# Splitting the first part's weights by tap halves, so that four passes can leave out an image row

## The chip, the cores and the metric

One core of one Trainium2 chip. The metric is the time of one execution on the device in microseconds; the median of three runs of the kernel before is 2496.78 us (2495.84 to 2496.85).

## The reference

Input `x` is (4, 32, 32, 16): four images of 32 x 32 pixels with 16 channels. Four residual layers are applied, each to a group-normalised copy of `x`. Three of them (layers 0, 1 and 3) are of this kind:

```python
first = einsum('ijyx,byxc->bijc', M, inputs)
kern = ...                       # G: for each pixel (i,j) its own 3x3 kernel, 16 -> 16 channels
shifted = conv(inputs, kern)     # (b, i, j, y, x, f): 1024 convolutions of the whole image
diff = relu(inputs[:, None, None] - shifted)
second = einsum('ijyx,bijyxc->bijc', W, diff)
x = x + first - second
```

The third kind (layer 2, "interval") pools over intervals of the image with running maxima and minima and makes two small dynamic-programming steps of sigmoid and maximum over 33 x 33 tables. What fills the time is `shifted`: for each of the 1024 pixels, 16 output channels and 4 images, a 3 x 3 x 16 convolution over 1024 places.

## The kernel before, in words

**Phases, steps, units.** The four images are two groups of two (`g`, `b`). A phase is one convolution layer on one group: six phases in the order (g0, L0), (g1, L0), (g0, L1), (g1, L1), (g0, L2), (g1, L2), where L2 is the reference's layer 3. A phase has 8 chunks `t` of 128 output pixels; a chunk has 32 steps, one for each channel `f` and image `b`. So a phase is 256 steps, and there are 1536 in all. Four channels' weights are a unit: eight steps use one unit. Units 0 and 1 ("plain") are used as loaded, by 16 steps; units from 2 on are split.

**What a step does on TensorE.** The nine taps' 16 channels are 144 input rows. The partitions' halves 0 to 63 and 64 to 127 hold the left and right half image (512 pixels each, two adjacent matmuls of 64 rows, one into each half of the PSUM pair). Each half has two slots `s` of four taps, 0 to 3 and 4 to 7; the ninth tap stands apart in `im9`. For accuracy in the fast matmul format, weights and images are split into an upper part (the top bits) and the rest. `first_part` makes four passes of 512 columns: `WU[s]` with `iy[s]` (upper weights with upper image x 2^-12) and `WL[s]` with `iz[s]` (the rests); ScalarE then scales the PSUM pair by 1 + 2^-12 (L627). `second_part`, one step later, adds `WD[s]` with `iyz[s]` and the ninth tap (496 columns; its last image row has nothing to add), and VectorE (L644) does minimum, product with W and sum into a column of `acc`. Four PSUM pairs are in turn. Layout by weights: `WU`, `WL`, `WD` are 128 x 512 tiles of `parts[:, 0]`; `parts[:, 1]` is a copy with the partition halves swapped, made by two DMAs on SP (L242).

**The order around it.** Each engine's order is the order in which this program emits. Each step of `conv_layer` takes one piece of `prep_parts` (eight pieces for a unit, thirteen steps ahead of its first use), then emits `first_part` of this step and `second_part` of the step before, then perhaps one piece of `behind`, the generator that prepares the next phase. A piece of `prep_parts` yields a tuple: at `IDLE` ScalarE has no weight work in that step, at `CALM` VectorE has none. A piece of `behind` that yields a number is followed by the next after so many steps; one that yields `IDLE` or `CALM` waits for a step whose tuple has it. Piece k of a unit falls on steps that are k + 2 modulo 8, so the step 0 of a phase has a piece 6. The pieces before: 1 VectorE's mask of the upper bits (`upper`, L198); 2 ScalarE's half of the ninth tap's weights (L172); 3 `WD` scaled on ScalarE (L231), `WL` by subtraction on POOL (L232), the ninth tap's sum on POOL (L233); 4 `WU` copied on ScalarE (L235), `WD` summed on POOL (L236); 5 the next unit's subtraction of ones on the diagonal (`prep`, L209); 7 the swapped copy (L242) and the load of raw weights two units on (L108). Their tuples have IDLE at 1, 5, 6, 7, 8 and CALM at 6, 7, 8.

**What is behind.** `before_conv` normalises the next group (`group_norm`: sums, pause `gap`, totals with two pauses `gap`, mean and squares on POOL, pause 4, sums, pause `gap`, IDLE, ScalarE's square-root table, two pauses `gap`, pause 2, IDLE, 1/deviation, pause 2, product, pause 3; `gap` is 4, in the last layer 1, in the interval layer 2), transposes it, writes it to DRAM (`xs`, L356, 8 DMAs) and reads it back in 24 DMAs (L367), two a step, as `raw`, one image row block for each tap. After a pause of 12 (6 in the last layer) `split` makes `iy` and `iz` for each of the two images and `difference` makes `iyz`. For `first` of the reference, `load_first_terms` loads M (4 MB, `MT`, two DMAs on SP, L385) and `first_terms` multiplies. `interval_layer` runs the interval layer for a group; its `step` adds 33 x 33 tables on POOL (L550) and takes maxima on VectorE, one row of tables every six steps.

**The shared buffer.** One buffer of 128 x 8192 float32 (pool `big`, `bufs=1`) holds in turn the plain units, `MT` and the interval layer's tables; a new tile there waits for the readers of the last.

**Queues.** All of the DMAs named go out on SP's queue, in the order of the program.

Of the kernel before, what the change touches and what calls it, by code (L numbers as in the profile page):

```python
# [15 lines left out]
P = 128  # L16
B, H, C = 4, 32, 16
NG = 2
# [11 lines left out]
LAST = (H - 1) * HW  # L30
ROWS = P // H
# [11 lines left out]
def net_kernel(ctx: ExitStack, tc: tile.TileContext, x, xq, xi, convs, iv_w, iv_b, out):  # L43
# [77 lines left out]
    iy = [const.tile([P, 2, GB, NH], F32R, name=f"iy{g}") for g in range(NG)]  # L121
    iz = [const.tile([P, 2, GB, NH], F32R, name=f"iz{g}") for g in range(NG)]
# [8 lines left out]
    plain = first[:, : PLAIN * 3 * FU * P].rearrange("p (u s f k) -> p u s f k", u=PLAIN, s=3, f=FU)  # L131
# [29 lines left out]
    pick = (ident[:, 4 * C : 5 * C], ident[:, :C])  # L161
# [21 lines left out]
    def zeros(g):  # L183

        nc.gpsimd.memset(xt[g], 0.0)
        for y in (0, HP - 1):
            nc.gpsimd.dma_start(
                xs[g][:, :, y * WP : (y + 1) * WP], zero[:GC].rearrange("p (h n) -> p h n", h=2)
            )

# [24 lines left out]
    def prep_parts():  # L215

        for u in range(PLAIN, n_chunks * NU):  # L220
            parts = wpool.tile([P, 2, 3, FU, P], F32R, tag="parts", bufs=AHEAD + 1, name=f"parts_{u}")
            W9 = wpool.tile([P, FU, P], F32R, tag="W9", bufs=AHEAD + 1, name=f"W9_{u}")
            units[u] = [parts[:, :, k] for k in range(3)] + [W9]
            src = raws.pop(u)
            w8 = src[:, 0].rearrange("p f k -> p (f k)")
            WU, WL, WD = (parts[:, 0, k].rearrange("p f k -> p (f k)") for k in range(3))
            high = upper(src[:, 0:1], 1, f"w{u}")[:, 0]
            yield (IDLE,)
            halve(W9, src[:, 1], low_w)
            yield ()  # L230
            nc.scalar.activation(WD, high, AF.Copy, scale=-EPS)  # L231
            nc.gpsimd.tensor_tensor(WL, w8, high, ALU.subtract)  # L232
            nc.gpsimd.tensor_tensor(W9, W9.bitcast(F32), src[:, 2], ALU.add)  # L233
            yield ()
            nc.scalar.copy(WU, high)  # L235
            nc.gpsimd.tensor_tensor(WD, WD.bitcast(F32), WL.bitcast(F32), ALU.add)  # L236
            yield ()
            prep(u + 1)
            yield (IDLE,)
            yield (IDLE, CALM)  # L240
            for h in range(2):
                nc.sync.dma_start(  # L242
                    parts[64 * h : 64 * h + 64, 1].bitcast(F32),
                    parts[64 - 64 * h : 128 - 64 * h, 0].bitcast(F32),
                )
            load_raw(u + RAWS)
            yield (IDLE, CALM)
            yield (IDLE, CALM)
# [12 lines left out]
    def split(eng, g, b, name, pause=IDLE):  # L261

        high = upper(image(raw[:, :2, b], WP), 2, f"x{name}{b}")
        yield 1
        for s in range(2):
            eng.tensor_tensor(
                image(iz[g][:, s, b], HW), image(raw[:, s, b], WP), image(high[:, s], HW), ALU.subtract
            )
            yield pause
            nc.scalar.activation(iy[g][:, s, b], high[:, s], AF.Copy, scale=EPS)  # L270

    def difference(eng, g, b, s):
        eng.tensor_tensor(
            iyz[g][:, s, b], iy[g].bitcast(F32)[:, s, b], iz[g].bitcast(F32)[:, s, b],
            ALU.subtract,
        )
# [66 lines left out]
    def before_conv(g, layer):  # L343
# [17 lines left out]
        for slot, row, tap in [(tap // 4, tap % 4, tap) for tap in range(8)] + [  # L361
            (2, row, 8) for row in range(4)
        ]:
# [7 lines left out]
        yield 6 if layer == 2 else 12  # L371
        for b in range(GB):
            yield from split(nc.gpsimd, g, b, f"{g}{layer}")
            yield IDLE
            halve(image(im9[g][:, b], HW), image(raw[:, 2, b], WP), low_x)
            for s in range(2):
                difference(nc.gpsimd, g, b, s)
            yield 3
# [211 lines left out]
    def products(ps, pairs, first, ninth=False):  # L590


        for k, (w, v) in enumerate(pairs):
            n = LAST if ninth and k == len(pairs) - 1 else NH
            for h in range(2):
                r = slice(64 * h, 64 * h + 64)
                nc.tensor.matmul(  # L597
                    ps[:, h, :n],
# [5 lines left out]
                )  # L604

    def first_part(step):
# [5 lines left out]
        if u < PLAIN:  # L612
# [4 lines left out]
                True, ninth=True,  # L617
# [5 lines left out]
            [(WU[:, s], iy[g][:, s, b]) for s in range(2)]  # L623
            + [(WL[:, s], iz[g][:, s, b]) for s in range(2)],
            True,
# [4 lines left out]
    def second_part(step, ps):  # L630
# [5 lines left out]
        if u >= PLAIN:  # L636
# [3 lines left out]
                False, ninth=True,  # L640
# [54 lines left out]
    def behind(phase):  # L695
# [7 lines left out]
        if phase + 1 < len(phases):  # L703
# [3 lines left out]
            terms = g1 == NG - 1 and layer1 < NL - 1  # L707
            if terms:
                mt = load_first_terms(layer1)
            yield from before_conv(g1, layer1)  # L710
            if terms:
# [24 lines left out]
    for b in range(GB):  # L736
# [9 lines left out]
        "left0": rows[:, 0, 0::3], "right0": rows[:, 1, 1:2],  # L746
        "top0": rows[:, 0, 0:3], "bottom0": rows[:, 1, 2:4],
        "left1": rows[:, 0, 2:3], "right1": rows[:, 1, 2:3],
        "top1": rows[:, 1, 0:3], "bottom1": rows[:, 0, 2:4],
# [83 lines left out]
    def rest_of_start():  # L833
# [14 lines left out]
        yield 2  # L848
        for b in range(GB):
            yield from split(nc.vector, 0, b, "00", 1)  # L850
            yield 1
            for s in range(2):
                difference(nc.vector, 0, b, s)
# [88 lines left out]
```

## Time and profile before

| | |
|---|---|
| median of 3 runs | 2496.78 us (2495.84 to 2496.85) |
| profiled execution, its own time | 2497.43 us |
| its span, first to last instruction | 2495.7 us, TensorE's granted clock 1.0 |
| TensorE busy | 2478.2 us (99%) |
| VectorE busy | 2081.2 us (83%) |
| ScalarE busy | 1882.6 us (75%) |
| POOL busy | 1103.0 us (44%) |
| share of the chain that ended last: TensorE, L597 | 94% |
| passes, L597: 512 columns, 64 rows | 6080 matmuls for each of iy, iz, iyz |
| passes, L597: 496 columns | 3072 matmuls |
| L644, VectorE, mean | 1224 ns, 1536 times |
| L627, ScalarE, mean | 1008 ns, 1520 times |

PE is TensorE's matmuls, PEld its weight loads, DVE VectorE, ACT ScalarE, SP the queue that issues the DMAs. Line numbers are those of the kernel. A busy share is an average over the span, and matmuls' ends are modelled, so that two passes can seem to overlap: the time of a pass is read from the distance of two starts.

### The profile page before, as it was taken

What the parts mean: (1) busy time and instruction counts of PE and PEld (TensorE: products, weight loads), DVE (VectorE), ACT (ScalarE), POOL (GpSimd) and SP (SyncE); (2) the same over time, 40 slices, a digit from 0 to 9 for tenths busy, and PEclk for the clock granted to TensorE, in tenths of its full rate; (3) what the DMA queues carried; (4) which work ended last, traced back from release to release, by engine and by line L of the source; (5) the groups of instructions that cost most, each with busy time, mean ns of one, the idle gap of its engine ahead of it and who ended that gap; (6) DMA issues with size and microseconds to landing.
All of it is one profiled execution on the core that took longest, in us unless ns stands there. A gap on an engine that the chain in (4) does not pass through costs nothing.

```text
span 2495.7 us, 56685 instructions
## 1 busy us (share of the span) xinstructions
PE 2478.2 (99%) x21906; PEld 2080.4 (83%) x21906; DVE 2081.2 (83%) x3617; ACT 1882.6 (75%) x2181; POOL 1103.0 (44%) x990
## 2 busy tenths in 40 slices
PE   8999999999999999999999999999999999999999
PEld 5899888888888888888888888888889888888887
DVE  9888788888888887888888988889889887788887
ACT  4777777787777777777777777787777777777776
POOL 3445333454343435433345555454646444333332
PEclk9999999999999999999999999999999999999999
DMA  5566445465444654544454444554444467354442
GB/s 176 184 150 178 116 136 143 114 177 141 132 142 133 200 160 123 140 134 133 134 144 136 136 119 138 146 159 134 125 138 137 133 167 202 114 145 136 136 136 54
DMA packets 86622, 354.43 MB, mean 142 GB/s; under 512 B 23888, under 2 KB 25808, under 8 KB 85584
## 3 DMA queue, kind: packets, MB, share of 16 engines
q1 hardware_dynamic: 85360, 350.21, 50.5%
q8 instruction: 172, 2.82, 0.5%
q14 instruction: 98, 0.80, 0.1%
q10 hardware_dynamic: 864, 0.58, 0.1%
q0 software_dynamic: 128, 0.02, 0.0%
HBM read 199.78 MB, written 1.02 MB: 80 GB/s over the span
## 4 chain that ended last, share of the span: by engine, by line
PE 95%; DMA 2%; DVE 1%; SPq 1%; issue 1%; ACT 1%; POOL 0%; DVEq 0%; ACTq 0%; POOLq 0%
PE pc L597 94%; DMA parts<-parts 1%; PE pf L395 1%; DMA raw<-in_g 1%; DVE junk L644 1%; SPq L367 0%; ACT pc L627 0%; SPq L356 0%; SPq L242 0%; PE ps_r L531 0%; PE ps_l L518 0%; DVE tables L478 0%; DMA xs<-xt 0%; ACT iy L270 0%; ACT L328 0%
## 5 line engine op out<-in xcount | busy, mean ns | idle before, releaser
L644 DVE SCALAR_TENSOR_TENSOR junk<-pc,WT 128x1024 f32<-128x1024 f32 x1536 | 1879.5, 1224 | 389.8 <-PE pc L597 347.0
L627 ACT ACTIVATE pc<-pc 128x1024 f32<-128x1024 f32 x1520 | 1531.8, 1008 | 578.4 <-PE pc L597 549.0
L597 PE MATMUL pc<-iy,parts 64*128 64x512 f32 x6080 | 957.3, 387 | 3.8 <-DMA parts<-parts 3.2
L597 PE MATMUL pc<-iyz,parts 64*128 64x512 f32 x6080 | 954.0, 387 | 2.3 <-ACT pc L627 2.2
L597 PE MATMUL pc<-iz,parts 64*128 64x512 f32 x6080 | 953.5, 386 | 0.0
L597 PEld LDWEIGHTS pc<-iyz,parts 64*128 64x128 f32 x6080 | 589.3, 184 | 110.4 <-ACT pc L627 6.1
L597 PEld LDWEIGHTS pc<-iy,parts 64*128 64x128 f32 x6080 | 590.2, 184 | 106.1 <-DMA parts<-parts 5.4
L597 PEld LDWEIGHTS pc<-iz,parts 64*128 64x128 f32 x6080 | 591.7, 184 | 104.4
L232 POOL TENSOR_TENSOR parts<-raw,upper_w 128x512 fp32r<-128x512 f32 x190 | 246.5, 1297 | 965.6 <-PE pc L597 808.8
L597 PE MATMUL pc<-im,W 64*128 64x496 f32 x3072 | 609.5, 384 | 0.0
L597 PEld LDWEIGHTS pc<-im,W 64*128 64x128 f32 x3072 | 301.2, 184 | 56.5 <-issue 3.5
L233 POOL TENSOR_TENSOR W<-W,raw 128x512 fp32r<-128x512 f32 x190 | 247.3, 1301 | 1.6 <-ACT W L172 1.6
L236 POOL TENSOR_TENSOR parts<-parts 128x512 fp32r<-128x512 f32 x190 | 246.6, 1298 | 1.9 <-ACT parts L231 1.9
L209 POOL TENSOR_TENSOR raw<-raw,ident 128x512 f32<-128x512 f32 x190 | 200.7, 1056 | 80.6 <-DMA raw<-in_g 80.5
L172 ACT ACTIVATE W<-raw,low_w 128x512 fp32r<-128x512 f32 x190 | 136.0, 716 | 0.1
L644 DVE DVE_READ_ACCUMULATOR junk<-pc,WT 128x1 f32 x1536 | 127.3, 83 | 0.0
L231 ACT ACTIVATE parts<-upper_w 128x512 fp32r<-128x512 f32 x190 | 118.6, 624 | 4.4 <-DVE upper_w L198 4.2
L235 ACT CAST parts<-upper_w 128x512 fp32r<-128x512 f32 x190 | 116.8, 615 | 0.0
L198 DVE TENSOR_SCALAR upper_w<-raw 128x512 int32<-128x512 int32 x190 | 82.1, 432 | 0.4 <-POOL raw L209 0.2
L659 POOL TENSOR_SCALAR acc<-acc 128x32 f32<-128x32 f32 x40 | 11.9, 297 | 151.4 <-DVE junk L644 146.8
L550 POOL TENSOR_TENSOR tables<-ft_b,rt 128x1089 f32<-128x1089 f32 x16 | 37.7, 2359 | 0.0
L550 POOL TENSOR_TENSOR tables<-ft_a,rt 128x1089 f32<-128x1089 f32 x16 | 37.7, 2359 | 0.0
(136 smaller groups left out, 397.3 us busy)
## 6 DMA issues: line engine op xcount, KB each, us to landing
raw<-in_g SPq DMA_DIRECT2D x190, 768.0 KB, 7.1
parts<-parts SPq DMA_DIRECT2D x380, 384.0 KB, 5.0
WT<-in_w SPq DMA_DIRECT2D x48, 512.0 KB, 4.8
MT<-in_mt SPq DMA_DIRECT2D x6, 2048.0 KB, 14.2
raw<-xs SPq DMA_DIRECT2D x120, 71.8 KB, 2.8
raw<-in_xi SPq DMA_DIRECT2D x3, 287.0 KB, 4.7
raw<-in_xi SPq DMA_DIRECT2D x1, 861.0 KB, 6.8
xs<-xt SPq DMA_DIRECT2D x40, 18.0 KB, 1.7
```

The source lines that it names most:

```text
L172: nc.scalar.activation(dst, src, AF.Copy, scale=mask[:, 1:2])
L198: nc.vector.tensor_scalar(t.bitcast(I32), src.bitcast(I32), HIGH, None, op0=ALU.bitwise_and)
L209: eng.tensor_tensor(raws[u][:, s, at:to], raws[u][:, s, at:to], pick[s][:, f0 + at : f0 + to].unsqueeze(2).to_broadcast([P, to - at, P]), ...
L231: nc.scalar.activation(WD, high, AF.Copy, scale=-EPS)
L232: nc.gpsimd.tensor_tensor(WL, w8, high, ALU.subtract)
L233: nc.gpsimd.tensor_tensor(W9, W9.bitcast(F32), src[:, 2], ALU.add)
L235: nc.scalar.copy(WU, high)
L236: nc.gpsimd.tensor_tensor(WD, WD.bitcast(F32), WL.bitcast(F32), ALU.add)
L550: nc.gpsimd.tensor_tensor(t, ft[:, i, :].unsqueeze(1).to_broadcast([P, T1, T1]), rt, ALU.add,)
L597: nc.tensor.matmul(ps[:, h, :n], lhsT=w[r], rhs=v[r] if n == NH else v[r][:, :n], start=first and k == 0, stop=k == len(pairs) - 1, skip_g ...
L627: nc.scalar.activation(ps, ps, AF.Copy, scale=1.0 + EPS)
L644: nc.vector.scalar_tensor_tensor(junk, ps.rearrange("p h n -> p (h n)"), 0.0, chunks[n], op0=ALU.min, op1=ALU.mult, accum_out=accs[phase][ ...
```

## The change

The taps' order becomes `TAPS`: slot 0 has the taps 0 to 3, slot 1 the taps 6, 7, 4, 5. In the first part's passes a group of 64 rows no longer holds four taps' upper (or lower) parts, but the upper and lower parts of two taps: `WU` holds taps 0, 1 (slot 0) or 6, 7 (slot 1) with `ia`, `WL` the taps 2, 3 or 4, 5 with `ib`. Taps 0 and 1 belong to the row above, 6 and 7 to the row below: in the passes of `WU` the outer row of the half is left out, 496 columns instead of 512. The passes of `WL` come first. The weights' quarters of 32 partitions are put together on POOL and ScalarE: two subtractions and one copy on POOL and one copy on ScalarE more for each unit, and the pieces' order differs; the swapped copy goes with piece 8, IDLE is at pieces 1, 4, 7, 8 and CALM at 4, 7, 8. The images' upper and lower parts are made in a temporary tile (in `big`) and placed into `ia` and `ib` by 12 DMAs for each image (`place`). `MT` of the first two layers is loaded after `before_conv` instead of ahead of it, with a pause of 24 steps before `first_terms`.

```diff
+TAPS = ((0, 1, 2, 3), (6, 7, 4, 5))
+TEMP = 2 * 2 * GB * NH
...
+    QUARTERS = [(slice(64 * h, 64 * h + 32), slice(64 * h + 32, 64 * h + 64)) for h in range(2)]
...
             high = upper(src[:, 0:1], 1, f"w{u}")[:, 0]
             yield (IDLE,)
-            halve(W9, src[:, 1], low_w)
+            nc.scalar.copy(WU, high)
+            nc.gpsimd.tensor_tensor(WL, w8, high, ALU.subtract)
+            for lo, hi in QUARTERS:
+                nc.gpsimd.tensor_tensor(WU[hi], w8[lo], high[lo], ALU.subtract)
             yield ()
             nc.scalar.activation(WD, high, AF.Copy, scale=-EPS)
-            nc.gpsimd.tensor_tensor(WL, w8, high, ALU.subtract)
+            nc.gpsimd.tensor_tensor(WD, WD.bitcast(F32), WL.bitcast(F32), ALU.add)
+            yield ()
+            yield (IDLE, CALM)
+            halve(W9, src[:, 1], low_w)
             nc.gpsimd.tensor_tensor(W9, W9.bitcast(F32), src[:, 2], ALU.add)
             yield ()
-            nc.scalar.copy(WU, high)
-            nc.gpsimd.tensor_tensor(WD, WD.bitcast(F32), WL.bitcast(F32), ALU.add)
+            (lo0, hi0), (lo1, hi1) = QUARTERS
+            nc.scalar.copy(WL[lo0], high[hi0])
+            nc.gpsimd.tensor_copy(WL[lo1], high[hi1])
+            prep(u + 1)
             yield ()
-            prep(u + 1)
-            yield (IDLE,)
             yield (IDLE, CALM)
             for h in range(2):
                 nc.sync.dma_start(
...
             load_raw(u + RAWS)
-            yield (IDLE, CALM)
             yield (IDLE, CALM)
...
+    def place(engs, g, b, temp):
+        ty, tz = (v.bitcast(F32) for v in halves(temp, b))
+        da, db = (v[g].bitcast(F32)[:, :, b] for v in (ia, ib))
+        k = 0
+        for h, (lo, hi) in enumerate(QUARTERS):
+            for s in range(2):
+                at = HW if s == h else 0
+                for to, src in ((lo, ty), (hi, tz)):
+                    engs[k % len(engs)].dma_start(da[to, s, :LAST], src[lo, s, at : at + LAST])
+                    k += 1
+            for to, src in ((lo, ty), (hi, tz)):
+                engs[k % len(engs)].dma_start(db[to], src[hi])
+                k += 1
+            yield 1
...
         yield 6 if layer == 2 else 12
+        temp = big.tile([P, 8192], F32R, tag="big", name=f"temp_{g}{layer}")[:, :TEMP]
         for b in range(GB):
-            yield from split(nc.gpsimd, g, b, f"{g}{layer}")
+            yield from split(nc.gpsimd, g, b, temp, f"{g}{layer}")
             yield IDLE
             halve(image(im9[g][:, b], HW), image(raw[:, 2, b], WP), low_x)
+            yield from place([nc.sync], g, b, temp)
             for s in range(2):
-                difference(nc.gpsimd, g, b, s)
-            yield 3
+                difference(nc.gpsimd, g, b, s, temp)
+            yield 1
...
-            [(WU[:, s], iy[g][:, s, b]) for s in range(2)]
-            + [(WL[:, s], iz[g][:, s, b]) for s in range(2)],
-            True,
+            [(WL[:, s], ib[g][:, s, b]) for s in range(2)]
+            + [(WU[:, s], ia[g][:, s, b]) for s in range(2)],
+            True, {2 + s: without_outer(s) for s in range(2)},
...
             terms = g1 == NG - 1 and layer1 < NL - 1
+            yield from before_conv(g1, layer1)
             if terms:
                 mt = load_first_terms(layer1)
-            yield from before_conv(g1, layer1)
-            if terms:
+                yield 24
                 yield from first_terms(layer1, mt)
...
+        temp = first.bitcast(F32R)[:, used : used + TEMP]
         for b in range(GB):
-            yield from split(nc.vector, 0, b, "00", 1)
-            yield 1
+            yield from split(nc.vector, 0, b, temp, "00", 1)
+            yield from place([nc.sync, nc.scalar], 0, b, temp)
             for s in range(2):
-                difference(nc.vector, 0, b, s)
+                difference(nc.vector, 0, b, s, temp)
             yield 1
```

In `products`, `without_outer(s)` gives a half's matmul 496 columns that begin at 16 in the half h = s and at 0 in the other. The host packs G and the first images in the order of `TAPS`.

## The prediction

> **What bounds the kernel now.** I read the page's busy shares first, then the chain that ended last.
>
> ```profile
> PE 2478.2 (99%) x21906; PEld 2080.4 (83%) x21906; DVE 2081.2 (83%) x3617; ACT 1882.6 (75%) x2181; POOL 1103.0 (44%) x990
> PE 95%; DMA 2%; DVE 1%; SPq 1%; issue 1%; ACT 1%; POOL 0%; DVEq 0%; ACTq 0%; POOLq 0%
> ```
>
> TensorE is busy throughout and holds 95% of the chain: a column taken from a pass is time, if nothing else makes TensorE wait. The timeline of TensorE (start us, duration, what) gives the price of a column.
>
> ```profile
> 1001.18 0.62 PE L597 MATMUL pc<-iy,parts 64*128 64x512 f32 x4
> 1001.64 0.62 PE L597 MATMUL pc<-iz,parts 64*128 64x512 f32 x4
> 1002.09 0.62 PE L597 MATMUL pc<-iyz,parts 64*128 64x512 f32 x4
> 1002.54 0.38 PE L597 MATMUL pc<-im,W 64*128 64x496 f32 x2
> 1002.76 0.62 PE L597 MATMUL pc<-iy,parts 64*128 64x512 f32 x4
> ```
>
> The two halves' matmuls start together, so a line with x4 is two passes. Six passes of 512 columns take 1002.54 - 1001.18 = 1.36 us, 0.227 each; the one of 496 takes 0.22. Sixteen columns are 6.7 ns, and a step is 1.58 us.
>
> Next the timeline of one weight unit (eight steps, 12.64 us), since the change gives POOL and ACT more to do for each.
>
> ```profile
> 1217.48 0.42 DVE L198 TENSOR_SCALAR upper_w<-raw 128x512 int32<-128x512 int32 x1
> 1218.03 1.30 POOL L232 TENSOR_TENSOR parts<-raw,upper_w 128x512 fp32r<-128x512 f32 x1 [7.84 <-PE pc L597]
> 1218.10 0.71 ACT L172 ACTIVATE W<-raw,low_w 128x512 fp32r<-128x512 f32 x1
> ...
> 1219.29 1.29 POOL L233 TENSOR_TENSOR W<-W,raw 128x512 fp32r<-128x512 f32 x1
> 1220.54 1.29 POOL L236 TENSOR_TENSOR parts<-parts 128x512 fp32r<-128x512 f32 x1
> 1221.78 1.04 POOL L209 TENSOR_TENSOR raw<-raw,ident 128x512 f32<-128x512 f32 x1
> 1221.99 1.10 SPq L242 DMA_DIRECT2D parts<-parts  x2
> ```
>
> I count from L198's start, called t. POOL's links begin 1.26 us apart from t = 0.55; the swap of halves (L242) is issued at t = 4.5 and lands 5.0 us later by the page's median. POOL is idle 7.84 us per unit, ACT 0.57 us ahead of most L627.
>
> Last, the place where TensorE does wait for a swap: SP's, VectorE's and TensorE's timeline at the last load of MT.
>
> ```profile
> 2067.57 2.07 SPq L385 DMA_DIRECT2D MT<-in_mt  x2
> 2069.91 0.42 DVE L198 TENSOR_SCALAR upper_w<-raw 128x512 int32<-128x512 int32 x1
> 2074.43 1.11 SPq L242 DMA_DIRECT2D parts<-parts  x2
> 2089.04 0.61 PE L597 MATMUL pc<-iy,parts 64*128 64x512 f32 x3
> 2091.01 0.50 PE L597 MATMUL pc<-iy,parts 64*128 64x512 f32 x1 [1.37 <-DMA parts<-parts]
> ```
>
> The swap was issued at t = 4.5 as always, but behind 4 MB of MT it landed 16.0 us later, 23.4 us after MT's issue. TensorE needed it for its second pass, at 2089.04 + 0.23, which is t = 19.4, and lost 1.7 us. The other two MT loads (issued at 109.02 and 822.73) show swaps that took up to 14.2 and 11.7 us; no stall followed, because MT had gone out right behind the swap before.
>
> **What is removed.** In 1520 steps, two passes lose 16 columns: 1520 x 2 x 6.7 ns = 20.3 us. That the shortened passes are shorter in fact, the 496-column row shows.
>
> **A unit's chain.** POOL gets two quarter subtractions and a quarter copy. A quarter has as many elements per partition as L232, so I take 1.26 us each for the subtractions and 1.0 for the copy (L209: 1.04); bounds 0.6 and 2.36 (L550, 1089 elements). The new chain: WL 0.55 to 1.81, two quarters to 4.3, WD to 5.6, W9 to 7.3 (its ACT half, three steps behind the first, ends at 6.0), copy to 8.3, the next unit's L209 to 9.4. All fits in 12.6 us; if it did not, its 3.5 us on 190 units would be 665 us. ACT's extra quarter copy (0.61, from L235) lies in the 0.57 us gap ahead of an L627, as L235 does now without delaying any; uncovered it would be 116 us. But the swap moves from t = 4.5 to 8.4 and lands at 14.5, not 10.6, due at 19.2: spare time falls from 8.8 to 4.7 us. And ACT's copy into WL, the fourth step after the first (t = 0.6 + 4 x 1.57 = 6.9), must wait until POOL's WD sum (end 5.6) has read WL: a new wait with 1.3 us to spare. Behind it in ACT's queue is the scaling L627, and behind that TensorE's second part; L627 ends 0.36 us before it is needed (1218.76 + 1.01 against 1220.13).
>
> VectorE and POOL side by side: L644 has a spread of only 1189 to 1227 ns over 1536 calls, whether POOL runs or not, so I charge nothing. One rule speaks against that: the Trainium skill (GPSIMD Engine Reference, Key points) says that POOL shares its SBUF interfaces with VectorE and contends with instructions in a two-port mode or with two SBUF inputs. If L644 were such an instruction, 3.5 us more of POOL per unit against VectorE's 0.35 us of idle per step would cost some (3.5 - 2.8) x 190 = 133 us; L644 reads one input from PSUM, and the row decides for nothing.
>
> **Where POOL is late for ACT.** I counted the yields. Step 0 of a phase is the sixth piece of a unit; in phases 0 and 2 the group norm's pauses (4 each, and IDLE pieces now 1, 4, 7, 8) put the second image's differences behind piece 2, so 2 x 1.3 us go ahead of the WD sum. It ends at 8.2, ACT is held 1.3 us, TensorE 1.3 - 0.36 = 0.9. The same count gives one such place in each of the five prepared images' phases: 4.7 us. In the interval layers' first step an L550 (2.36 us) stands behind piece 2 twice per layer: 4 x (2.36 - 1.3 - 0.36) = 2.8. Sum 7.5, bounds 0 (quarters at 0.6) and 12; I take 6.
>
> **The placing copies.** 12 per image on SP, 24 a phase, at L242's 0.55 us: 6.6 us of SP per image, ahead of swaps or behind them. Their landing lets the differences' buffer go; nothing on TensorE waits for them within 10 steps. Cost through the swap: 0 to 2 us a phase, inside the next item. In the start phase half go to ACT's queue (six of 0.35 to 0.57 us an image) while TensorE runs the plain units; 0.5 us, bounds -1 and 2.
>
> **The stretches of xs reads.** Five times, 24 L367 fill SP's queue; there the swaps go out up to 15 us after L198 (513.12 against 498.97) and land just at the due time: most of the page's 8.6 us of TensorE waiting for parts outside MT. The swap stands one piece later, so behind two to four more L367 of 0.45 us: 1 to 2 us in each stretch. I take 6 us, bounds 0 and 12.
>
> **MT moves.** It now needs the buffer of the temporary images, so it goes after them. The same count puts it, in phases 0 and 2, at piece 4 of a unit (steps 150 and 598), two steps behind the differences and four ahead of that unit's swap. SP reaches it when the buffer is free: between t = 6.9 (POOL's end of the differences) and 10.3 (placing copies behind a raw load). I take 8.5. The swap, ready at 11, is in SP's order behind MT. From the three MT loads now, a swap behind MT lands 22.5 to 23.4 us after MT's issue; there a raw load had gone 1.2 us ahead, here it is older, so I take 20.5, with 18.3 (MT's own landing) as lower end. Landing: 29.0, due 19.2, stall 9.8. Bounds 6 and 14.5. Two of them: 19.6 us (12 to 29). They are hidden by nothing: TensorE has no other work in its order. The 24 steps (38 us) given to MT do cover its own landing. At the last phase MT keeps its place, but the swap before it is later by up to 3.9 us: 1.5 us more (0 to 4).
>
> **The sum**, against the profiled execution's 2497.43 us (span 2495.7): - 20.3 + 19.6 + 6 + 6 + 1.5 + 0.5 = + 13.3, so 2510.7. The median of the runs is 0.65 lower: 2510.
>
> **Rivals.** (1) Faster: the swap behind MT does land in time. It decides from a landing below t = 19.2, that is if the swap's packets pass MT's. For it: 14.2 us is not 18.3, and two loads of three cost nothing. Against: they were issued after the swap before. Then the 19.6 is 0, the other terms 6 to 14: 2497.4 - 20.3 + 6 to 14, less 0.65, 2482 to 2491. (2) The waits are half of what I took, and gain and loss cancel: 2492 to 2502. (3) POOL's quarters cost 2.2 us (like L550): WD ends at 7.5, ACT is late in every unit by 0.6, TensorE by about 0.25 on 190 units: 47 us more, 2557. For it: only that no 32-partition operation of this size is in the trace.
>
> **How the numbers follow.** My forecast (both MT stalls, the small waits) has 0.64, own range 2502 to 2524; rival 1 0.13, rival 2 0.17, rival 3 0.06. The bound of what can be told is 0.2%, 5 us: faster 0.13, same 0.17, slower 0.64 + 0.06 = 0.70. The range 2492 to 2524 leaves out rivals 1 and 3, about 2 in 10.
>
> **What would show it.** TensorE's rows for the first part's two shortened forms start 0.22 apart; two waits of 6 to 14 us for the parts swap, 25 to 30 us after L198, right behind MT near 260 and 1000 us; TensorE's waits for ACT up from 8.3 us; L242 issued at t = 8.4. I am wrong if no wait for parts follows MT, or if L242 comes at t > 10 in an ordinary unit.

## The result, and the profile after

The changed kernel takes 2572.64 us (median of 5 runs, 2569.19 to 2573.68) against 2496.78 (2495.84 to 2497.15): ratio 1.0302, 95% interval 1.0287 to 1.0317. It is slower by 75.9 us where 13.3 had been forecast; the profiled span is 2570.9 us, 75.2 longer. The direction was right, the size far outside the range.

The page's busy times and its chain that ended last:

```profile
PE 2491.1 (97%) x21906; PEld 2061.6 (80%) x21906; DVE 2092.3 (81%) x3617; ACT 1989.8 (77%) x2371; POOL 1731.6 (67%) x1560
...
PE 81%; DMA 6%; DVE 4%; issue 4%; ACT 3%; POOL 3%; SPq 0%; ACTq 0%; DVEq 0%; POOLq 0%
```

TensorE held 95% of the chain and holds 81%: the path now runs through DMAs, VectorE, ScalarE and POOL. (TensorE's busy time is no lower although columns are gone: part of it ran at half clock, see below.) The saving itself is there. TensorE's timeline of an undisturbed step:

```profile
1233.82 0.62 PE L628 MATMUL pc<-ib,parts 64*128 64x512 f32 x4
1234.27 0.60 PE L628 MATMUL pc<-ia,parts 64*128 64x496 f32 x4
1234.71 0.62 PE L628 MATMUL pc<-iyz,parts 64*128 64x512 f32 x4
1235.17 0.38 PE L628 MATMUL pc<-im,W 64*128 64x496 f32 x2
1235.39 0.62 PE L628 MATMUL pc<-ib,parts 64*128 64x512 f32 x4
```

The two shortened passes (four matmuls of 64 rows, two for each half image) take 1234.71 - 1234.27 = 0.44 us, 0.22 each; the step 1235.39 - 1233.82 = 1.57 us. Over the whole trace the mean distance from one pass's start to the next, waits left out, is 0.2270 us behind 512 columns and 0.2203 behind 496: 6.7 ns for 16 columns.

POOL's part of the same unit, with the swap on SP:

```profile
1231.09 1.30 POOL L235 TENSOR_TENSOR parts<-raw,upper_w 128x512 fp32r<-128x512 f32 x1 [3.90 <-DVE upper_w L203]
1232.46 2.63 POOL L237 TENSOR_TENSOR parts<-raw,upper_w 32x512 fp32r<-32x512 f32 x2
1235.17 1.29 POOL L240 TENSOR_TENSOR parts<-parts 128x512 fp32r<-128x512 f32 x1
...
1237.98 0.61 POOL L248 CAST parts<-upper_w 32x512 fp32r<-32x512 f32 x1
1238.62 2.47 SPq L253 DMA_DIRECT2D parts<-parts  x2
```

In an ordinary unit things are nearly as reckoned: a quarter subtraction costs what a whole one costs (two in 2.63 us), the copy 0.61, the swap goes out 7.5 us after L235's start (forecast 7.85), and POOL is still idle for 3.9 us. What was lost was lost elsewhere. The table of waits (who waited for whom: us in total, times, longest), first before:

```profile
PEld pc L597 <- ACT pc L627: 6.1, 10, 0.8
...
PEld pc L597 <- DMA parts<-parts: 5.4, 5, 1.7
...
ACT parts L231 <- DVE upper_w L198: 4.2, 2, 2.1
```

and after:

```profile
PEld pc L628 <- ACT pc L664: 65.6, 81, 4.3
...
PEld pc L628 <- DMA parts<-parts: 36.9, 13, 11.5
PE pc L628 <- ACT pc L664: 34.8, 39, 3.9
...
PE pc L628 <- DMA parts<-parts: 31.4, 11, 11.1
ACT parts L234 <- DVE upper_w L203: 28.0, 30, 2.8
ACT parts L247 <- POOL parts L240: 24.5, 17, 2.4
```

By the sums that the prediction took (PEld and PE together, which wait side by side, so that no time lost can be read from them) waits for parts went from 8.6 to 68.3 us and waits for ACT from 8.3 to 100.4. The last two rows, of ACT, are where its lateness begins: L247 is the wait that the prediction named, L234 one that it did not.

From the trace I summed what the distances of neighbouring matmuls' starts have above 222 ns and sorted them by what held the second (ScalarE's by its longest idle time in the 4.5 us ahead), before and after. The rows of MT are exact to 0.1 us; the others, ScalarE's above all, move by 1 to 2.5 us with the rule of sorting:

| term | forecast | after less before |
|---|---|---|
| 16 columns in two passes | -20.3 | -20.3 (by the spacing) |
| two MT stalls | +19.6 | +25.6 |
| last MT | +1.5 | +2.9 |
| stretches of xs reads | +6 | +1.7 |
| ScalarE late | +6 | +37.4 (L247 19.3, L234 14.7, ScalarE merely busy 3.4) |
| start | +0.5 | +4.2 |
| TensorE at half clock | not named | +9.6 |
| passes right behind a wait | not named | +7.5 |
| sum | +13.3 | +68.6, of 75.2; 6.6 not assigned |

**MT.** The timeline of SP and TensorE at the first MT:

```profile
264.74 1.59 SPq L110 DMA_DIRECT2D raw<-in_g  x1
...
270.58 4.34 SPq L300 DMA_DIRECT2D ia<-temp  x4
274.96 1.29 SPq L303 DMA_DIRECT2D ib<-temp  x2
278.04 0.81 SPq L416 DMA_DIRECT2D MT<-in_mt  x2
...
278.96 1.15 SPq L253 DMA_DIRECT2D parts<-parts  x2
...
297.31 0.79 PE L628 MATMUL pc<-ib,parts 64*128 64x512 f32 x1 [10.40 <-DMA parts<-parts]
...
298.92 0.79 PE L628 MATMUL pc<-ib,parts 64*128 64x512 f32 x1 [0.82 <-DMA parts<-parts]
```

MT stands between two swaps, as forecast. The swap behind it landed 18.3 us after its issue and TensorE lost 10.6 and 1.4 us by those distances; at the second MT 11.3 and 2.4.

**ScalarE behind POOL.** Where the group norm runs, from the timeline:

```profile
70.13 0.26 POOL L348 TENSOR_SCALAR mean_c<-whole_mc 128x16 f32<-128x16 f32 x1 [5.21 <-DVE whole_mc L341]
...
71.80 1.30 POOL L235 TENSOR_TENSOR parts<-raw,upper_w 128x512 fp32r<-128x512 f32 x1
...
73.18 2.63 POOL L237 TENSOR_TENSOR parts<-raw,upper_w 32x512 fp32r<-32x512 f32 x2
...
75.89 1.30 POOL L240 TENSOR_TENSOR parts<-parts 128x512 fp32r<-128x512 f32 x1
...
77.22 0.62 ACT L247 CAST parts<-upper_w 32x512 fp32r<-32x512 f32 x1 [1.99 <-POOL parts L240]
...
78.79 0.73 PE L628 MATMUL pc<-iyz,parts 64*128 64x512 f32 x4 [1.48 <-ACT pc L664]
```

POOL stood 5.21 us for VectorE's L341 and did three small operations (L348, L350, L352) before the unit's chain could begin at 71.80. ScalarE's copy waited 1.99 us for the WD sum, the scaling L664 stood behind it, and TensorE waited 1.48.

**ScalarE behind the mask.** Another place, in the interval layer:

```profile
1995.53 2.35 POOL L581 TENSOR_TENSOR tables<-ft_b,rt 128x1089 f32<-128x1089 f32 x1
...
1995.78 2.38 DVE L203 TENSOR_SCALAR upper_w<-raw 128x512 int32<-128x512 int32 x1
...
1998.19 0.62 ACT L234 CAST parts<-upper_w 128x512 fp32r<-128x512 f32 x1 [1.76 <-DVE upper_w L203]
...
1999.78 0.73 PE L628 MATMUL pc<-iyz,parts 64*128 64x512 f32 x4 [1.26 <-ACT pc L664]
```

A mask of 0.42 us took 2.38 beside POOL's L581 and ended 0.28 us after it. The copy into WU now follows the mask by one step; before, that step held the ninth tap's half, which needs no mask.

### The profile page after: what moved, and what is told of

Its sections match the earlier page's. It is cut to its first block, busy times and chain, and to the rows that moved or that the text cites. A ratio compares the mean times of both kernels' runs of the same rounds, so it can differ in the third digit from the quotient of the medians.

```text
span 2570.9 us, 57968 instructions
## 1 busy us (share of the span) xinstructions
PE 2491.1 (97%) x21906; PEld 2061.6 (80%) x21906; DVE 2092.3 (81%) x3617; ACT 1989.8 (77%) x2371; POOL 1731.6 (67%) x1560
## 4 chain that ended last, share of the span: by engine, by line
PE 81%; DMA 6%; DVE 4%; issue 4%; ACT 3%; POOL 3%; SPq 0%; ACTq 0%; DVEq 0%; POOLq 0%
PE pc L628 79%; DMA parts<-parts 4%; DVE junk L681 3%; ACT pc L664 2%; DMA raw<-in_g 1%; POOL parts L237 1%; PE pf L426 1%; POOL parts L240 1%; DMA WT<-in_w 1%; POOL parts L235 0%; DVE upper_w L203 0%; DMA raw<-in_xi 0%; POOL iyz L289 0%; POOL W L244 0%; POOL tables L581 0%
## 5 line engine op out<-in xcount | busy, mean ns | idle before, releaser
L681 DVE SCALAR_TENSOR_TENSOR junk<-pc,WT 128x1024 f32<-128x1024 f32 x1536 | 1879.7, 1224 | 451.1 <-PE pc L628 411.8
L664 ACT ACTIVATE pc<-pc 128x1024 f32<-128x1024 f32 x1520 | 1529.3, 1007 | 476.5 <-PE pc L628 467.7
L628 PE MATMUL pc<-iyz,parts 64*128 64x512 f32 x6080 | 973.1, 391 | 35.7 <-ACT pc L664 34.8
L628 PE MATMUL pc<-ib,parts 64*128 64x512 f32 x6080 | 972.3, 389 | 32.0 <-DMA parts<-parts 31.4
L628 PE MATMUL pc<-ia,parts 64*128 64x496 f32 x6080 | 944.7, 381 | 0.0
L628 PEld LDWEIGHTS pc<-ib,parts 64*128 64x128 f32 x6080 | 595.7, 185 | 145.4 <-DMA parts<-parts 36.9
L628 PEld LDWEIGHTS pc<-iyz,parts 64*128 64x128 f32 x6080 | 584.5, 185 | 153.7 <-ACT pc L664 65.6
L628 PEld LDWEIGHTS pc<-ia,parts 64*128 64x128 f32 x6080 | 596.8, 185 | 111.4
L628 PE MATMUL pc<-im,W 64*128 64x496 f32 x3072 | 617.8, 385 | 0.0
L235 POOL TENSOR_TENSOR parts<-raw,upper_w 128x512 fp32r<-128x512 f32 x190 | 246.2, 1296 | 548.5 <-DVE upper_w L203 448.3
L237 POOL TENSOR_TENSOR parts<-raw,upper_w 32x512 fp32r<-32x512 f32 x380 | 490.7, 1291 | 28.8 <-ACT parts L234 3.3
L244 POOL TENSOR_TENSOR W<-W,raw 128x512 fp32r<-128x512 f32 x190 | 247.8, 1304 | 36.1 <-ACT W L175 34.4
L214 POOL TENSOR_TENSOR raw<-raw,ident 128x512 f32<-128x512 f32 x190 | 198.0, 1042 | 82.7 <-DMA raw<-in_g 58.5
L234 ACT CAST parts<-upper_w 128x512 fp32r<-128x512 f32 x190 | 118.3, 623 | 35.5 <-DVE upper_w L203 28.0
L247 ACT CAST parts<-upper_w 32x512 fp32r<-32x512 f32 x190 | 118.0, 621 | 30.9 <-POOL parts L240 24.5
L681 DVE DVE_READ_ACCUMULATOR junk<-pc,WT 128x1 f32 x1536 | 127.3, 83 | 0.0
L248 POOL CAST parts<-upper_w 32x512 fp32r<-32x512 f32 x190 | 116.7, 614 | 12.3
L239 ACT ACTIVATE parts<-upper_w 128x512 fp32r<-128x512 f32 x190 | 118.1, 621 | 5.9 <-DVE iyz L289 5.9
L203 DVE TENSOR_SCALAR upper_w<-raw 128x512 int32<-128x512 int32 x190 | 89.0, 468 | 0.9 <-POOL raw L214 0.7
```

The costliest lines, as they stand in the source:

```text
L214: eng.tensor_tensor(raws[u][:, s, at:to], raws[u][:, s, at:to], pick[s][:, f0 + at : f0 + to].unsqueeze(2).to_broadcast([P, to - at, P]), ...
L237: nc.gpsimd.tensor_tensor(WU[hi], w8[lo], high[lo], ALU.subtract)
L247: nc.scalar.copy(WL[lo0], high[hi0])
L628: nc.tensor.matmul(ps[:, h, at : at + n], lhsT=w[r], rhs=v[r] if n == NH else v[r][:, :n], start=first and k == 0, stop=k == len(pairs) - ...
L664: nc.scalar.activation(ps, ps, AF.Copy, scale=1.0 + EPS)
L681: nc.vector.scalar_tensor_tensor(junk, ps.rearrange("p h n -> p (h n)"), 0.0, chunks[n], op0=ALU.min, op1=ALU.mult, accum_out=accs[phase][ ...
```

## The experiments

Ratios are to the kernel before, which ran beside each version on the same chip; brackets are 95% intervals. Gains in us are differences of medians, mostly to the changed kernel's 2572.64. The kernel before took 2496.8 to 2497.7 on all the chips used, while the runs of one version spread by 1 to 10 us.

| version | us | ratio |
|---|---|---|
| cut alone, in the kernel before | 2483.31 | 0.9948 [0.9931, 0.9964] |
| MT's new place alone, in the kernel before | 2497.62 | 1.0000 [0.9990, 1.0010] |
| change, MT behind the swap | 2551.10 | 1.0212 [1.0195, 1.0229] |
| change, MT in quarters | 2539.08 | 1.0164 [1.0149, 1.0179] |
| change, both copies on POOL | 2567.97 | 1.0281 [1.0265, 1.0297] |
| change, quarters of WU copied | 2558.31 | 1.0243 [1.0229, 1.0257] |
| change, ninth tap first | 2559.32 | 1.0246 [1.0230, 1.0261] |
| change, start's copies on SP | 2575.93 | 1.0313 [1.0295, 1.0330] |
| MT in quarters + ninth first | 2517.75 | 1.0078 [1.0063, 1.0093] |
| the same, three edits more | 2501.34 | 1.0017 [1.0008, 1.0026] |
| those, and the start on SP | 2496.06 | 0.9993 [0.9984, 1.0001] |
| and the swap on POOL, behind L214 | 2505.03 | 1.0035 [1.0021, 1.0049] |
| or on POOL, ahead of L214 | 2506.59 | 1.0037 [1.0024, 1.0050] |
| or on SP, two pieces earlier | 2484.67 | 0.9949 [0.9936, 0.9963] |

### The columns by themselves

In the kernel before, the two passes over `iz` leave out their last 16 columns; nothing else changes.

```diff
-            n = LAST if ninth and k == len(pairs) - 1 else NH
+            n = LAST if ninth and k == len(pairs) - 1 or first and not ninth and k > 1 else NH
```

> The kernel before, with the two passes of iz cut to 496 columns and nothing else changed (it leaves out the last image row of those passes). Theory (a column is 0.417 ns, TensorE is the bound): 1520 x 2 x 6.7 = 20.3 us off, 2476.5 us. Rival (another engine is just behind TensorE, so that the columns are worth less): 2485 or more.

2483.31 (2481.76 to 2490.46): 14.4 us gained, between the theory and its rival. The profile, of the fastest run, has longer waits near 2025 us, where the kernel before lost 0.9 us:

```profile
2023.24 0.50 PE L597 MATMUL pc<-iy,parts 64*128 64x512 f32 x1 [0.84 <-DMA parts<-parts]
2025.02 0.79 PE L597 MATMUL pc<-iy,parts 64*128 64x512 f32 x1 [1.28 <-DMA parts<-parts]
```

And its windows view right behind (from:to, us, busy of PE, PEld, DVE, ACT, POOL, granted clock, DMA share, GB/s):

```profile
2025.02:2028.43 3.41, 3.41 (x16) 2.79 (x18) 0.43 (x1) 1.01 (x1) 0.33 (x1) 0.50 0.92 281
```

16 matmuls in 3.41 us, at half clock (0.50). Waits and half clock cost some 3.6 us. The profiled span is 15.7 us shorter, 19.3 with those given back, so the saving is nearly the 20.3 that was reckoned. But a faster TensorE brings the same swaps closer to their due times.

### MT

First, MT's new place alone, in the kernel before (no buffer to wait for):

```diff
+            yield from before_conv(g1, layer1)
             if terms:
                 mt = load_first_terms(layer1)
-            yield from before_conv(g1, layer1)
-            if terms:
+                yield 24
                 yield from first_terms(layer1, mt)
```

> The kernel before, with only MT's move: in phases 0 and 2 it is loaded after the preparation of the images, 24 steps ahead of its use; the images are made as before, with no temporary tile. Theory (MT comes between swap and swap because it must wait until the temporary tile is free; where nothing holds the buffer, SP reaches it right behind the last raw load, as before): 2496 to 2500. Rival (the place in the program's order alone makes the swap late): 2510 to 2520.

2497.62, no difference. There MT goes out at 234.17, right behind a swap (231.77) and 9.4 us ahead of the next. The place in the program costs nothing; the wait for the buffer of the temporary images does, because it carries MT to within a microsecond of the swap that comes after it.

Second, in the changed kernel, MT four steps later, so that it goes out behind that swap:

```diff
+                yield 4
                 mt = load_first_terms(layer1)
```

> The changed kernel, with a pause of 4 more steps ahead of MT's load, so that in phases 0 and 2 it stands behind a unit's swap (piece 8) instead of ahead of it (piece 4). Theory (the swap is late because it is queued behind 4 MB): the two stalls of TensorE of 12 to 14 us and the half clock behind them go, save for 1 to 2 us each: 26 to 32 us off 2572.6, so 2541 to 2547, and granted clock near 0.996. Rival (the stall is the shorter lead of the swap, wherever MT stands): 2565 or more.

2551.10, 21.5 us gained, short of the 26 to 32 expected. The stalls of 12.0 and 13.6 us shrank to 1.6 and 3.7. They did not vanish: the next swap still landed 12 to 15 us after its issue behind 4 MB. At the last MT, whose place is the same, the loss grew from 4.5 to 6.6. Third, MT as four loads of 1 MB, eight steps apart, each behind a swap, in the last phase too:

```diff
-        for half in range(2):
-            nc.sync.dma_start(mt[:, NT // 2 * half : NT // 2 * (half + 1)], convs[layer][0][half])
+        for q in range(4):
+            nc.sync.dma_start(
+                mt[:, 2 * q : 2 * q + 2], convs[layer][0][q // 2][:, q % 2 * 2 : q % 2 * 2 + 2]
+            )
+            yield 8
```

> The changed kernel with each MT load in four DMAs of 1 MB, eight steps apart, each right behind a unit's swap and raw load; in the last phase too. Theory (a swap is late by what is queued ahead of it): no TensorE stall for parts behind MT, all three gone, and no half clock but the start's: 24 to 34 us off 2572.6, so 2539 to 2549, and 3 to 8 below the kernel that only moved MT behind the swap (2551). Rival (MT's 4 MB cost the same wherever they go): 2550 or more.

2539.08, 33.6 us gained, as expected (24 to 34). Its waits for parts:

```profile
PEld pc L631 <- DMA parts<-parts: 10.6, 9, 2.1
```

So MT, with the half clock and the passes behind its stalls, was worth 33.6 of the 96 us that the change lost beside its 20.3 us of gain; I had 21.1.

### ScalarE's two waits

The wait of L247 for POOL can be taken from ScalarE by giving the copy to POOL:

```diff
-            nc.scalar.copy(WL[lo0], high[hi0])
+            nc.gpsimd.tensor_copy(WL[lo0], high[hi0])
```

> The changed kernel, with both quarter copies into WL on POOL, so that ScalarE no longer waits for POOL's sum of WD. Theory (that wait costs TensorE 17 stalls, 19 us): 2550 to 2556, and no wait of ScalarE for POOL L240. Rival (the same lateness reaches TensorE another way, by the swap that POOL now issues 0.6 us later): 2568 or more.

2567.97, at most a few us gained (the intervals overlap): a miss. ScalarE no longer waits for POOL, but what was lost came back in other rows: L234's share grew from 14.7 to 21.7 us and waits for parts from 36.1 to 42.7.

Next the chain's length. `WU`'s quarters have the values that `WL` has just received, so they can be copied:

```diff
-                nc.gpsimd.tensor_tensor(WU[hi], w8[lo], high[lo], ALU.subtract)
+                nc.gpsimd.tensor_copy(WU[hi], WL[lo])
```

> The changed kernel with one edit: the two quarters of WU are copied from WL's quarters, which hold the same values (so far 614 ns for a 32x512 copy on POOL), and no longer subtracted a second time (1291 ns). POOL's chain up to the sum of WD is 1.35 us shorter in each of 190 units; the order of everything else stands. Theory (ScalarE's copy into WL waits for a POOL that is late by the chain's length, 17 sites of 1.1 us each): most of the 19.3 us behind L247 goes, the masks' 14.7 us and the MT stalls stay: 2553 to 2561 us. Rival (POOL is late because group norm and tables stand ahead of the chain, its length does not matter, or the lateness moves on to the swap): 2567 us or more.

2558.31 (2550.77 to 2560.62), 14.3 us gained, within what was expected. ScalarE's waits in its profile, which is of the fastest run:

```profile
ACT parts L234 <- DVE upper_w L203: 27.0, 30, 2.7
...
ACT parts L247 <- POOL parts L240: 4.1, 7, 0.7
```

The wait for POOL fell from 24.5 to 4.1, the one for the mask stayed. The first was the chain's length on top of POOL's late start.

Then the order: the ninth tap first, which needs no mask, and L247's copy last, on POOL:

```diff
+            halve(W9, src[:, 1], low_w)
+            nc.gpsimd.tensor_tensor(WL, w8, high, ALU.subtract)
+            yield ()
             nc.scalar.copy(WU, high)
-            nc.gpsimd.tensor_tensor(WL, w8, high, ALU.subtract)
...
+            nc.gpsimd.tensor_tensor(W9, W9.bitcast(F32), src[:, 2], ALU.add)
...
-            nc.scalar.copy(WL[lo0], high[hi0])
+            nc.gpsimd.tensor_copy(WL[lo0], high[hi0])
```

> The changed kernel with the pieces' order changed: piece 2 has the ninth tap's ScalarE half and POOL's WL, piece 3 the WU copy and POOL's quarters and the ninth tap's sum, piece 5 WD, piece 6 both copies into WL on POOL. So ScalarE's first operation of a unit no longer needs VectorE's mask of one step before, and none waits for POOL. Theory (two new waits of ScalarE, for POOL and for VectorE, delay the scaling L664: 19 and 15 us): ScalarE's waits for VectorE's mask fall from 28 us to under 8, TensorE's waits for ScalarE from 100 us to under 25, and the time to 2535 to 2550. Rival (with the copies on POOL alone the lateness only moved on to the swap, 4.7 us gained; it will again): 2560 or more.

2559.32, 13.3 us gained, between the theory and its rival. The waits show why not more:

```profile
PEld pc L628 <- DMA parts<-parts: 53.5, 19, 14.7
...
PEld pc L628 <- DVE junk L681: 21.9, 37, 1.4
...
PEld pc L628 <- ACT pc L664: 17.4, 25, 5.2
...
DVE upper_w L203 <- POOL raw L214: 15.9, 23, 2.2
```

Waits for ACT fell from 65.6 to 17.4. In their place VectorE now waits for POOL's L214 in the next unit's mask, TensorE for VectorE, and the MT stalls grew from 12.0 and 13.6 to 16.6 and 15.5 us.

### The start

```diff
-            yield from place([nc.sync, nc.scalar], 0, b, temp)
+            yield from place([nc.sync], 0, b, temp)
```

> The changed kernel, with the start's placing copies on SP's queue alone. Theory (six copies in ScalarE's queue wait for a landing, and the weights' scaling of unit 3 stands behind them): the stall of 4.0 us near 45 us and the half clock behind it (about 3 us) go: 2565 to 2567. Rival (the copies land too late on either queue): 2570 to 2573.

2575.93, ratio 1.0313 against the change's 1.0302 with intervals that overlap: no gain that can be told, a miss. The trace shows the expected one in the first 100 us (5.9 us less lost there than in the changed kernel), but PEld's waits for parts grew from 36.9 to 44.3 us, at the xs reads and the last MT. That the swaps there have no margin is likely; why they landed later in this run is not settled.

### Putting the mends together

MT in quarters and the ninth tap first, as above:

> The changed kernel with both: MT in quarters and the pieces' order with the ninth tap first. If the two causes are apart, the gains add: 2572.6 less 30 less 30 is 2512, range 2500 to 2520. If mending the one only uncovers the other: 2530 or more.

2517.75: 54.9 us gained, more than 33.6 + 13.3 = 46.9: the grown MT stalls of the ninth-first order are gone as well. Then, with the quarters of WU copied as above, WL's two copies right behind the WD sum, L214 a piece later and the swap a piece earlier:

```diff
             nc.gpsimd.tensor_tensor(WD, WD.bitcast(F32), WL.bitcast(F32), ALU.add)
-            yield ()
             (lo0, hi0), (lo1, hi1) = QUARTERS
             nc.gpsimd.tensor_copy(WL[lo0], high[hi0])
             nc.gpsimd.tensor_copy(WL[lo1], high[hi1])
+            yield ()
             prep(u + 1)
             yield ()
-            yield (IDLE, CALM)
             for h in range(2):
                 nc.sync.dma_start(
...
             yield (IDLE, CALM)
+            yield (IDLE, CALM)
```

> The version with MT in quarters and the ninth tap first, with three edits more: the quarter copies of the run beside it, WL's own quarter copies right behind the sum of WD with the next unit's L214 a piece later, and the swap a piece earlier in SP's order. Of the 56 us that TensorE still lost there 16.9 were waits for parts in the stretches of xs reads (a swap a piece earlier stands ahead of 2 to 4 reads of 0.45 us) and 12.6 waits for VectorE. Theory (both are a matter of the chain's length and the swap's place): half of the 16.9 and a few of the 12.6 us go, 2502 to 2512 us, above the kernel before by less than 0.6%. Rival (the waits for VectorE stay and the swap is held by its data, not by its place): 2514 us or more.

2501.34, a little better than the 2502 to 2512 expected. And the start on SP:

> As the run beside it, with the start's placing copies on SP's queue alone and none on ScalarE's. In the version with MT in quarters 4.3 us of waits behind ScalarE's held queue and 4.7 us of half clock were left at 40 to 55 us. Theory (the start's loss is ScalarE's queue, held by a copy; in the changed kernel the same edit did cut the start's loss by 6 us, but waits for parts elsewhere rose by 8): with MT in quarters nothing is near the edge elsewhere, and 4 to 8 us are gained on the run beside it, 2496 to 2506 us. Rival (moving twelve DMAs between queues shifts landings elsewhere whatever the margins): no gain or a loss on the run beside it.

2496.06, 5.3 us better: with MT out of the way the start's gain stays. The change's price is now paid back, and no more. What is left by the waits of its profile (of the fastest run): PEld for parts 7.8 us, for VectorE 11.6, for ACT 13.3. By the distances the waits for parts lost 6.8 us; the expectations below go by 9.5.

### What held the last swaps

Is it SP's queue, or the swap's own data? First the swap issued from POOL, where L214 of the next unit stands ahead of it (so not right behind the copies, as the expectation has it); then with its issue ahead of L214; then on SP, in that earlier place.

```diff
-                nc.sync.dma_start(
+                nc.gpsimd.dma_start(
```

> The version with every mend (MT in quarters, ninth tap first, quarter copies, the start on SP) and one edit more: the swap of halves is issued from POOL, right behind the copies that it waits for, and no longer from SP, where it stands behind the xs reads. The four DMAs that POOL issues so far (xs<-zero) took 0.55 to 0.71 us each to issue and landed after 2.2 us. Theory (what is left of the waits for parts, 9.5 us and some 3 us of passes behind them, is SP's queue ahead of the swap): 8 to 12 us below the version without it (2496.06), 2484 to 2489 us, below the kernel before by 0.3 to 0.5%. Rival (POOL gives 1.1 us more per unit to the two issues, which makes its L214 and with it the mask and ScalarE's half late, or its queue lands later): 2494 us or more.

2505.03, 9 us worse: a miss. POOL's timeline in a stretch of xs reads:

```profile
1600.15 0.61 POOL L247 CAST parts<-upper_w 32x512 fp32r<-32x512 f32 x1
1604.22 1.04 POOL L214 TENSOR_TENSOR raw<-raw,ident 128x512 f32<-128x512 f32 x1 [3.46 <-DMA raw<-in_g]
1605.20 0.62 POOL L252 DMA_DIRECT2D parts<-parts  x1
1608.05 0.51 POOL L252 DMA_DIRECT2D parts<-parts  x1 [2.22 <-issue]
```

The data were ready at 1600.76; the swap stood behind L214, which waited for a raw load that the swap does not need, and its second half was held 2.22 us more.

The swap's place moved ahead of L214, in the next two runs:

```diff
             nc.gpsimd.tensor_copy(WL[lo1], high[hi1])
+            for h in range(2):
+                nc.gpsimd.dma_start(
...
             yield ()
             prep(u + 1)
             yield ()
-            for h in range(2):
...
```

> As the version with every mend and the swap issued from POOL, but with the swap's two issues ahead of the next unit's L214 in POOL's order, right behind WL's quarter copies. In the run before, L214 stood ahead of the swap and waited up to 3.46 us for its raw load in a stretch of xs reads, so the swap was held by a load that it does not need. Theory (in the stretches the swap is held by what stands ahead of it in its queue, reads or L214, not by its own data): the waits for parts fall from 14 us to under 5, 2488 to 2495 us. Rival (the swap's data are late themselves, since L235 and the masks come late there, or L214 now late by the two issues costs TensorE waits for VectorE): 2499 us or more.

2506.59, no better, as the rival said. Its waits:

```profile
PEld pc L631 <- DVE junk L684: 24.4, 39, 2.0
...
DVE upper_w L203 <- POOL raw L214: 19.4, 25, 2.2
...
PEld pc L631 <- DMA parts<-parts: 7.2, 5, 2.5
```

Waits for parts are little lower than on SP (7.8; the two longest here, 2.2 and 1.7 us by distance, are at the first MT and no longer in a stretch of reads), while two issues of 0.54 us ahead of L214 make the mask late and with it VectorE.

The same place, with `nc.sync.dma_start` as before (two pieces, and so four reads, earlier than in the version with the start on SP):

> As the version with every mend, the swap still on SP's queue but a piece earlier in the program, right behind WL's quarter copies: in a stretch two to four reads of 0.45 us that stood ahead of it stand behind it. Theory (SP's queue ahead of the swap): half of the 9.5 us of waits for parts goes, 2490 to 2494 us. Rival (the swap's data are not ready then either; SP now waits for them and the reads and loads behind it are held): 2496 us or more.

2484.67, more than expected. What is left of PEld's waits for parts:

```profile
PEld pc L631 <- DMA parts<-parts: 0.8, 2, 0.4
```

The 7.8 us of waits for parts are down to 0.8, the others stand (for VectorE 11.8, for ACT 12.8). In the stretches the swap had been held by the reads ahead of it in SP's queue: near 505 us its copies had ended at 506.5 and it went out at 512.55; here they end at 504.8 and it goes out at 507.15. This version beats the kernel before by 12.6 us, 0.51%, [0.37%, 0.64%].

## Why the prediction was right in sign and wrong in size

**The columns** were right, by the spacing and by the cut alone.

**The ordinary unit** was nearly right: the quarters stand 1.35 us apart (taken: 1.26), the copy takes 0.61 (1.0), the swap goes out at t = 8.1 (8.4), and all of it lies in POOL's idle time. Rival 3 fell with that.

**MT** was right in mechanism and place, and rivals 1 and 2 fell with it. The term was low: each pair of stalls was 12.0 and 13.6 us against 9.8. The failing input is the time at which MT goes out. I took t = 8.5 with 10.3 as the bound; it went out 12.2 and 14.6 us after the mask L203. SP's placing copies were themselves held by the raw load (the eighth of twelve went out at 273.11, when the load issued at 264.74 had landed), so that the last of them was out at t = 10.4 and 11.2. And MT then waited 1.7 and 3.2 us more for the last copy to land, which frees the buffer; the bound did not count that. Put into the sum the two times give 13.5 and 15.9; landing (17.7 to 20.9 us after MT, against 20.5) and due time took 1.5 to 2.2 back. And no term was there for what follows a stall, the half clock above all.

**"Where POOL is late for ACT"** is the step that failed: 6 us forecast, bound 12, measured 37. Two things in it were wrong. The count of late places took the differences and L550 only; the group norm's L348, L350 and L352, which wait for VectorE, stand ahead of the chain too, and so do more tables. There were 17 places, not 9, each about 1.1 us. And the change's move of the copy into `WU` from the fourth piece to the second was read as a change of POOL's work alone; it adds a wait of ScalarE for VectorE's mask, 30 times for 28.0 us, behind which L664 stands. The prediction listed ScalarE's waits for POOL and never asked where each ScalarE operation's own input is made, and how late that can be.

**VectorE and POOL side by side.** The row chosen, L644 (L681 after), was right about itself: 1227 ns at the longest in both kernels. But it was the wrong row. The mask's row says more:

```profile
L203 DVE TENSOR_SCALAR upper_w<-raw x190: 385/423/2380, 21.7 to 2533.8; 128x512 int32<-128x512 int32 x190
```

That is minimum, median and longest in ns; before, the longest was 1034. Of the 190 masks, 174 ran without POOL and took 428 ns at most. Of the 16 with POOL beside them, the 12 that began while a POOL operation was under way each ended 0.28 to 0.30 us behind the end of that operation and took 523 to 2380 ns; the four that had begun before POOL's operation took 416 to 423, and three times that operation, an L281, took 1.33 us where one alone took 1.22. So the one that came second was held. Of the 14.7 us lost behind L234, about half (7.7) stood behind 8 masks of over 500 ns. The Trainium skill's rule that was weighed and set aside (GPSIMD Engine Reference, Key points: POOL shares its SBUF interfaces with VectorE and contends with instructions in a two-port mode or with two SBUF inputs) agrees with this if the mask, which has one SBUF input, runs in a two-port mode; which mode it runs in no row shows. L681, with one input from PSUM, was not held.

**xs reads**: 6 forecast, 1.7 measured. ScalarE's lateness elsewhere slowed TensorE and may have hidden some of it, which no run shows by itself: as the lateness was mended, these waits came up (6.8 us of lost time in the version with the start on SP), and there the swap's place in SP's queue was the cause, as the prediction had it.

**The start**: bound 2, measured 4.2 and a spell of half clock. In ScalarE's queue one placing copy was held until 44.15 us, when a raw load issued on SP at 34.65 had landed (44.13), and L239 stood behind it:

```profile
44.15 0.65 ACTq L303 DMA_DIRECT2D ib<-first  x1
44.85 0.63 ACT L239 ACTIVATE parts<-upper_w 128x512 fp32r<-128x512 f32 x1 [5.91 <-DVE iyz L289]
```

The prediction priced the issues (0.35 to 0.57 us) and not the time for which a queue can hold the engine that issues from it.

## What to carry to other kernels

A saving on the bounding engine is worth its full size only if everything that feeds it keeps its margin; price each moved operation by asking, in its new place, where its input is made, what that engine does just before, and who stands behind it in its own queue. Sort a stretch's waits by place, not by the average unit: here the ordinary unit was nearly as reckoned, and nearly the whole loss fell in a few dozen places where something else was under way. When one wait is mended the next one comes up, so mends are to be tried together before a change is given up: this one went from 3.0% slower to 0.5% faster.

## What the runs showed that I had not expected

TensorE's clock can halve after waits, short ones too. At the first MT stall the windows view of the changed kernel reads:

```profile
290.60:304.30 13.70, 6.17 (x27) 4.62 (x29) 1.23 (x2) 1.79 (x2) 1.14 (x2) 0.50 1.01 223
```

The granted clock was 0.50 for 13.65 us, of which TensorE had work for the last 5.4. The spells last 3.41 us or multiples of it, but for the one at the end of each run. The Trainium skill (TensorE: Matmul & The Clock Gate, What's actually happening) has the array throttled after at least one idle window of about 3.4 us. The length of the spells agrees; the idle time needed does not: in the cut alone the spell of 3.41 us followed waits of 0.84 and 1.28 us, and the measurement decides. The kernel before had a wait of 1.37 us at its last MT and no such spell, so not every wait brings one.

The DMAs of SP and ScalarE hold one another by their count. In the traces of all the runs here, 591 to 971 of these DMAs each, none went out before the one eight issues ahead of it, on whichever of the two queues, had landed, and at most seven were under way at an issue. That is how a raw load held the placing copy at 273.11, ScalarE's copy at 44.15 and, in the stretches, the reads with the swap behind them. In the traces eight semaphores tell of these DMAs' landings; whether the limit is theirs was not tried. So a DMA's place in the order is also counted in what stands eight ahead of it.

A copy on POOL of 32 x 512 took 614 ns, the subtraction of the same shape 1291, as much as one of 128 x 512.
